# Forming a layer's expert sums in expert rows and scattering them to the tokens, in a two-layer attention and expert kernel

## The chip, the cores and the metric

The kernel runs on one core of one Trainium2 chip. The metric is the device time of one launch in microseconds, as the median of several runs. A profile is one execution of the same program, taken by the hardware profiler. The engines are called PE (TensorE, the matrix unit), DVE (VectorE), ACT (ScalarE), POOL (GpSimd) and SP (SyncE, which only issues transfers). Each of them carries out its own instructions in order, and waits in place when an operand is not there yet.

## The reference

800 tokens (8 batches of 100) of 512 numbers pass through four stages, each added to `x`: causal attention, experts with GELU, attention over tokens and context, and experts with SiLU. The change concerns the two expert stages, cut here to what counts:

```python
# layer 0
xf = xn.reshape(-1, d)                                  # xn: layer norm of x
probs = softmax(xf @ Wg.T + bg)
tp, ti = top_k(probs, 2);  tp = tp / (sum(tp) + 1e-8)
h = gelu(einsum('td,efd->tef', xf, W1) + b1)
y = einsum('tef,edf->ted', h, W2) + b2
out = sum over the two experts of tp * y                # added to xn and to x

# layer 1
top_vals, top_idx = top_k(x @ w_router, 2);  rw = softmax(top_vals)
h = silu(x @ w_gate) * (x @ w_up)
y = h @ w_down
out = sum over the two experts of rw * y
out = (out - mean(out)) * rsqrt(var(out) + 1e-5)        # over the 512 numbers of a token
x = x + out * ln_gamma + ln_beta
```

Every token is computed by its two best experts out of eight; the sum needs both of its answers, and in layer 1 the norm needs the sum.

## The kernel before

The kernel lays 800 tokens out in seven tiles of 128 partitions, the first with 32 tokens (`rows`, `starts`, lines 71 and 72). It goes through attention 0, experts 0, attention 1 and experts 1.

*Routing* (`Route`, line 219). `group` finds the two best experts of a few tiles of tokens, ranks every token in its two experts and gives it a row in each: `where[0]` and `where[1]` are row numbers in a table of 8 x 800 rows. The tokens are then scattered by indirect transfers into `sent`, a table of that shape in DRAM. `order` (line 292) sorts the experts by their load. Slot 0 of the loop that follows is the expert with the most tokens, and so on; `slot` holds each expert's slot.

*The loop over experts* (`work_off`, line 397). Eight slots run one after the other with capacities of 256, 240, 228, 220, 204, 200, 184 and 176 rows. For each slot, `arrived` fetches its rows from `sent` in two pieces on GpSimd's queue (`xg`), and TensorE turns them (`ps_tp`). `hidden1` (line 980) computes eight pieces of the hidden layer, each from 4 matmuls into `ps_g` and 4 into `ps_u`, ScalarE's SiLU, and VectorE's product `h` (line 995). The PSUM tiles `ps_g` and `ps_u` have two buffers each. After the first four pieces `between()` calls `send_back` of the slot before. `products` (line 366) then runs 64 matmuls into `ps_y`; the first eight of them need the eight pieces of `h` one after the other. `returned` (line 386) turns the answers back (`ps_yt`), copies them by VectorE to `y` and writes them to the table `answers` in DRAM in two pieces on GpSimd's queue. The second write waits for the first, since both address the table by a row known only at run time.

*Weights.* Pieces of 1 MB come on SyncE's queue into eight buffers (`Weights`, line 43). A piece is asked for as soon as a buffer is free: two when the first half of the hidden layer is done, two when the second is, two when the products are.

*What follows the loop.* If an expert has more tokens than its capacity, `rest` (line 412) works off the remainder under a branch. In layer 0 (lines 734 to 757) the part `project_early` projects five heads of context keys and values for the next attention, while for every token tile the two answers are fetched by indirect transfers (`fetch`, `back0`), added to `x` with their weights `m1` and `m2`, and the sum is normed (`moments`, `factors`, `scaled`) and turned into `xT1`, from which the next attention starts with `ps_col`. In layer 1 (lines 1019 to 1036) the two answers of each tile are fetched (`back1`), summed into `acc`, normed, multiplied by `gain`, added to `x`, which already has `bias` in it (line 967, in `fetch_gains`), and written to the output by SyncE.

The order of instructions on each engine is not the order of the source alone: a scheduler of the framework places them when the program is built. Transfers issued by GpSimd use eight completion semaphores in turn.

Of the kernel before, what the change touches and what calls it, by code (L numbers as in the profile page):

```python
# [38 lines left out]
GROUPS = ((0, 2), (2, 4), (4, 6), (6, NTILE))  # L39
SHORT = NT - NT // P * P  # L40
# [26 lines left out]
def two_layers(ctx: ExitStack, tc: tile.TileContext, a: dict, out: bass.AP):  # L67
# [144 lines left out]
    answers = dram.tile([ROWS, D], F32, name="answers")  # L212
    kept_keys = dram.tile([len(KEPT), P, S], F32, name="kept_keys")
# [5 lines left out]
    class Route:  # L219


        def __init__(self, layer, psum, tag):
            self.layer, self.psum, self.tag = layer, psum, tag
            self.logits = routes.tile([P, NTILE, NE], F32, tag="logits", name=f"logits{layer}")
            nc.vector.memset(self.logits, 0.0)
            self.m = [routes.tile([P, NTILE], F32, tag=f"m{k}", name=f"m{k}_{layer}") for k in range(2)]
            self.where = [
                routes.tile([P, NTILE], mybir.dt.int32, tag=f"where{k}", name=f"where{k}_{layer}") for k in range(2)
            ]
            self.sel = routes.tile([P, NTILE, NE], F32, tag="sel", name=f"sel{layer}")  # L230
            nc.vector.memset(self.sel[:, 0, :], 0.0)
            self.before = routes.tile([P, NTILE + 1, NE], F32, tag="before", name=f"before{layer}")
            nc.vector.memset(self.before[:, 0, :], 0.0)
# [4 lines left out]
        def largest(self, v, m, name):  # L238

            g = v.shape[1]  # L240
            nc.vector.tensor_reduce(m, v, AX.X, ALU.max)
            at = self.temp([P, NTILE, NE], f"at{name}")[:, :g, :]
            nc.vector.tensor_tensor(at, v, over_experts(m), ALU.is_equal)
            nc.vector.tensor_tensor(at, at, rank.unsqueeze(1).to_broadcast([P, g, NE]), ALU.mult)
            first = self.temp([P, NTILE], "first")[:, :g]
            nc.vector.tensor_reduce(first, at, AX.X, ALU.max)
            nc.vector.tensor_tensor(at, at, over_experts(first), ALU.is_equal)
            return at

        def group(self, i0, i1, xn, held=()):  # L250
# [3 lines left out]
            at1 = self.largest(v, self.m[0][:, i0:i1], 1)  # L254
            other = self.temp([P, NTILE, NE], "other")[:, :g, :]
            nc.vector.scalar_tensor_tensor(other, at1, -3e38, v, ALU.mult, ALU.add)
            at2 = self.largest(other, self.m[1][:, i0:i1], 2)
# [16 lines left out]
            for k, at in enumerate((at1, at2)):  # L274
                pick = self.temp([P, NTILE, NE], "pick")[:, :g, :]
                nc.vector.tensor_tensor(pick, at, row, ALU.mult)
                place = self.temp([P, NTILE], "place")[:, :g]
                nc.vector.tensor_reduce(place, pick, AX.X, ALU.add)
                nc.vector.tensor_copy(self.where[k][:, i0:i1], place)
# [12 lines left out]
        def order(self, load):  # L292
# [7 lines left out]
            slot = self.temp([P, NE], "slot")  # L300
# [29 lines left out]

    def rows_of(table, layer, s, r, n):

        of_all = table.rearrange("(e r) d -> e r d", e=NE)
        return of_all[bass.ds(owner[layer][s], 1), r : r + n, :].rearrange("o r d -> (o r) d")
# [13 lines left out]

    def fetch(dst, where, i, k):
        w = rows[i]  # L350
        nc.gpsimd.indirect_dma_start(
            out=dst[:w, :], out_offset=None,
            in_=answers, in_offset=bass.IndirectOffsetOnAxis(ap=where[k][:w, i : i + 1], axis=0),
        )
# [42 lines left out]
    def work_off(jobs, arrive, hidden, product, send_back, first=None, midway=None):  # L397


        (x, raw), done = arrive(*jobs[0][:3]), None  # L400
        if first is not None:
            weights.load(first + 8, raw[:1, 0, :1])
        for k, (e, r0, n, w1, w2) in enumerate(jobs):
            h = hidden(e, n, x, w1, lambda: done and send_back(*done))
            if k + 1 < len(jobs):
                x, raw = arrive(*jobs[k + 1][:3])
            if midway is not None and k == 4:
                midway(raw)
            done = e, r0, n, product(e, n, h, w2)
        send_back(*done)  # L410

    def rest(more, work, first, second, bufs):

        v = nc.values_load(more[:1, :1], min_val=0, max_val=1)
        with tc.If(v > 0), tc.tile_pool(name="rest", bufs=bufs) as rp:

            def piece(w):
                t = rp.tile([P, 4, 512], F32, tag="r", name="wr")
                nc.sync.dma_start(out=t, in_=w())
                return t  # L420

            work([
                (e, r0, min(CAP, NT - r0), lambda g, e=e: first(piece, e, g), lambda g, e=e: second(piece, e, g))
                for e in range(NE) for r0 in range(CAPS[e], NT, CAP)
            ])

# [61 lines left out]
    with tc.tile_pool(name="a0", bufs=1) as ap, tc.tile_pool(name="a0w", bufs=3) as aw, tc.tile_pool(  # L488
# [19 lines left out]
        def fill(table):  # L508
            flat = table.rearrange("r d -> (r d)").rearrange("(p f) -> p f", p=P)
            n = ROWS * D // P  # L510
            for k in range(0, n, 1024):
                nc.sync.dma_start(out=flat[:, k : min(n, k + 1024)], in_=nil[:, : min(1024, n - k)])
# [3 lines left out]
        fill(answers)  # L516
        weights.load(W_L0F)
# [164 lines left out]
        nc.vector.tensor_tensor(m2, m2, s, ALU.mult)  # L682


    with f0, tc.tile_pool(name="f0w", bufs=2) as fw, tc.tile_pool(
# [29 lines left out]
        def work0(jobs, first=None, midway=None):  # L715
# [3 lines left out]
                lambda e, r0, n, yT: returned(0, e, r0, n, yT, fp, ps), first, midway,  # L719
            )  # L720

# [7 lines left out]
        ], W_L0F, fetch_context)  # L729
        rest(  # L730
            more, work0, lambda piece, e, g: piece(of(0, "W1", e, g)), lambda piece, e, g: piece(of(0, "W2", e, g)), 4
        )

        bo = fw.tile([P, D], F32, name="bo", bufs=1)
        nc.scalar.dma_start(out=bo, in_=a["bo"][0].partition_broadcast(P))
# [6 lines left out]
        xT1 = columns_tile("xT1")  # L742
        for i in range(NTILE):
            w = rows[i]
            both = fp.tile([P, 2, D], F32, tag="nil", name="back0", bufs=2)
            for k, m in enumerate((m1, m2)):
                y = both[:, k]
                fetch(y, where, i, k)
                nc.vector.scalar_tensor_tensor(
                    x[:w, i, :], y[:w], m[:w, i : i + 1], x[:w, i, :], ALU.mult, ALU.add  # L750
                )
            xn = fp.tile([P, D], F32, tag="mv", name="xn1", bufs=2)
            scaled(xn, x[:, i, :], *factors(moments(x[:, i, :], "a1"), "b", twice=True))
            to_columns(xT1, xn, starts[i], rows[i], ps, gamma1, beta1)
            nc.gpsimd.tensor_tensor(x[:, i, :], x[:, i, :], bo, ALU.add)
        weights.limit = len(pieces)
        weights.load(W_L1A + 8, y[:1, :1])
# [197 lines left out]
    with tc.tile_pool(name="f1", bufs=1) as fp, tc.tile_pool(name="f1w", bufs=2) as fw, tc.tile_pool(  # L955
# [3 lines left out]
        acc = fp.tile([P, NTILE, D], F32, name="acc")  # L959

        def fetch_gains(behind):

            for t, n in ((gain, "ln_gamma"), (bias, "ln_beta")):
                nc.gpsimd.tensor_copy(t[:1, :1], behind[:1, 0, :1])
                nc.gpsimd.dma_start(out=t, in_=a[n].partition_broadcast(P))
            for i in range(NTILE):
                nc.gpsimd.tensor_tensor(x[:, i, :], x[:, i, :], bias, ALU.add)
            nc.gpsimd.tensor_copy(acc[:1, 0, :1], behind[:1, 0, :1])
            nc.gpsimd.memset(acc[:, 0, :], 0.0)
# [30 lines left out]
        def work1(jobs, first=None, midway=None):  # L1000
            work_off(
                jobs, lambda e, r0, n: arrived(1, e, r0, n, fw, ps), hidden1,
                lambda e, n, h, wd: products(n, h, [wd(g) for g in range(NF // 4)], NF, fw, ps),
                lambda e, r0, n, yT: returned(1, e, r0, n, yT, fw, ps), first, midway,
# [8 lines left out]
        ], W_L1F, fetch_gains)  # L1013
        rest(
            more, work1, lambda piece, e, g: (piece(of(1, "w_gate", e, g)), piece(of(1, "w_up", e, g))),
            lambda piece, e, g: piece(of(1, "w_down", e, g)), 2,
        )

        for i in range(NTILE):
            w = rows[i]  # L1020
            for k, m in enumerate((m1, m2)):
                y = fw.tile([P, D], F32, tag=f"back{k}", name="back1")
                fetch(y, where, i, k)
                if k == 0:
                    nc.vector.tensor_scalar(acc[:w, i, :], y[:w], m[:w, i : i + 1], None, ALU.mult)
                else:
                    nc.vector.scalar_tensor_tensor(
                        acc[:w, i, :], y[:w], m[:w, i : i + 1], acc[:w, i, :], ALU.mult, ALU.add
                    )

        for i in range(NTILE):
            w = rows[i]
            scaled(acc[:, i, :], acc[:, i, :], *factors(moments(acc[:, i, :], "out"), "a"))
            nc.vector.tensor_tensor(acc[:, i, :], acc[:, i, :], gain, ALU.mult)
            nc.vector.tensor_tensor(x[:, i, :], x[:, i, :], acc[:, i, :], ALU.add)
            nc.sync.dma_start(out=y_out[starts[i] : starts[i] + w], in_=x[:w, i, :])
# [70 lines left out]
```

## Time and profile before

| | us |
|---|---|
| median of 3 runs | 1853.74 (1853.73 to 1857.28) |
| the profiled execution's own time | 1852.47 |
| its span in the profile | 1851.0 |
| experts of layer 0, and the attention's start after them | 252 to 634, then 689 |
| experts of layer 1, first `ps_g` to last `ps_yt` | 1513.8 to 1804.1 |

The page's table of engines gives, for each, the microseconds in which it was busy and the number of instructions. Timelines list, in order of time, start, length, engine, line of the kernel, operation, output and inputs, how many were merged, and in brackets how long the engine stood idle before and what ended that. The busy time of 40 slices shows where the holes lie:

```profile
PE   4999899999999969999999999999999959999990
PEclk9999899999999979999999999999999979999995
```

A digit is the busy share in tenths of a slice of 46.3 us, in the second row the granted clock. The last slice, and the fifteenth, are the stretches after the two loops over experts.

### The profile page before, as it was taken

The page shows a single profiled execution, that of the slowest core. Times are in us where ns is not written, and L with a number is a line of the kernel's source. Part 1 is how long each engine was busy: PE and PEld are TensorE (multiplying, and loading weights), DVE is VectorE, ACT ScalarE, POOL GpSimd, SP SyncE. Part 2 cuts the span into 40 slices and gives each one's busy share as a digit, 9 for nine tenths or more (in the row PEclk, how much of TensorE's full clock was granted, in tenths as well). Part 3 has the DMA queues.
Part 4 walks back from the last instruction along what each step waited for, and adds up shares of the span by engine and source line. Part 5 has one row for each costly group of instructions (what it writes and reads, how often), then busy time and mean ns, then how long its engine had stood idle before and what let it go on. Part 6 is the DMA issues. An engine that isn't in the chain of part 4 may idle for free.

```text
span 1851.0 us, 26473 instructions
## 1 busy us (share of the span) xinstructions
PE 1725.6 (93%) x10427; PEld 1305.7 (71%) x10427; DVE 583.7 (32%) x1467; ACT 465.5 (25%) x1390; POOL 159.5 (9%) x266
## 2 busy tenths in 40 slices
PE   4999899999999969999999999999999959999990
PEld 2455578999999835566666656666666649999990
DVE  3464510101111050254454424444344411111115
ACT  2365321111111141343333323333233310010110
POOL 4010210000000040000010000000000010030003
PEclk9999899999999979999999999999999979999995
DMA  9921294454556373031120111213110255565513
GB/s 369 407 78 54 88 343 164 169 193 174 201 199 234 136 256 113 17 97 45 62 71 5 5 35 6 37 10 56 5 6 4 28 201 204 180 218 196 200 62 116
DMA packets 74485, 233.31 MB, mean 126 GB/s; under 512 B 23178, under 2 KB 35582, under 8 KB 57958
## 3 DMA queue, kind: packets, MB, share of 16 engines
q1 hardware_dynamic: 52978, 183.42, 29.0%
q0 software_dynamic: 10048, 30.58, 5.2%
q10 hardware_dynamic: 11316, 17.43, 3.2%
q8 instruction: 86, 1.41, 0.3%
q14 instruction: 57, 0.47, 0.1%
HBM read 180.36 MB, written 51.04 MB: 125 GB/s over the span
## 4 chain that ended last, share of the span: by engine, by line
PE 65%; issue 20%; DMA 10%; DVE 3%; ACT 1%; POOL 0%; POOLq 0%; ACTq 0%; another core or an unknown queue 0%; DVEq 0%
PE ps_m L443 17%; PE ps_col L432 7%; DMA answers<-y 6%; PE ps_sc L808 5%; PE ps_g L989 4%; PE ps_u L989 4%; PE ps_av L858 4%; PE ps_y L374 4%; PE ps_v L890 3%; PE ps_ptA L837 3%; PE ps_o L906 3%; PE ps_mv L455 2%; PE ps_v L535 2%; DMA back<-answers,where 1%; PE ps_o L646 1%
## 5 line engine op out<-in xcount | busy, mean ns | idle before, releaser
L443 PE MATMUL ps_m<-cb,w 128*128 128x361 f32 x896 | 297.3, 482 | 0.0
L374 PE MATMUL ps_y<-h,w 128*128 128x256 f32 (+7 forms) x1536 | 280.5, 344 | 0.0
L374 PEld LDWEIGHTS ps_y<-h,w 128*128 128x128 f32 x1536 | 268.6, 190 | 7.9
L443 PEld LDWEIGHTS ps_m<-cb,w 128*128 128x128 f32 x896 | 169.4, 194 | 102.1 <-issue 14.0
L706 PE MATMUL ps_h<-xgT,w 128*128 128x256 f32 (+7 forms) x1024 | 187.5, 344 | 0.0
L706 PEld LDWEIGHTS ps_h<-xgT,w 128*128 128x128 f32 x1024 | 179.2, 190 | 5.3 <-ACT h L710 0.2
L814 ACT ACTIVATE pr<-ps_sc,m 100x822 f32<-100x822 f32 x128 | 120.0, 943 | 188.1 <-DVE m L812 94.9
L812 DVE TENSOR_REDUCE m<-ps_sc 100x1 f32<-100x822 f32 x128 | 123.8, 1009 | 46.5 <-PE ps_sc L808 46.5
L838 DVE COPY prT<-ps_ptA 128x500 f32<-128x500 f32 x128 | 82.1, 678 | 168.5 <-PE ps_ptA L837 168.5
L447 ACT COPY mT<-ps_m 128x361 f32<-128x361 f32 x128 | 59.0, 462 | 299.2 <-PE ps_m L443 273.8
L710 ACT ACTIVATE h<-ps_h,s_b 128x256 f32<-128x256 f32 (+7 forms) x128 | 56.1, 439 | 303.5 <-PE ps_h L706 303.5
L432 PE MATMUL ps_col<-xT,w 128*128 128x400 f32 x320 | 115.1, 518 | 1.6 <-ACT xT L180 1.6
L989 PE MATMUL ps_g<-xgT,w 128*128 128x256 f32 (+7 forms) x512 | 103.1, 344 | 0.0
L989 PE MATMUL ps_u<-xgT,w 128*128 128x256 f32 (+7 forms) x512 | 102.8, 344 | 0.0
L432 PEld LDWEIGHTS ps_col<-xT,w 128*128 128x128 f32 x320 | 61.9, 197 | 48.0 <-issue 4.5
L808 PE MATMUL ps_sc<-mT,qT 64*100 64x311 f32 (+1 forms) x512 | 93.1, 468 | 0.0
L989 PEld LDWEIGHTS ps_u<-xgT,w 128*128 128x128 f32 x512 | 90.7, 190 | 2.6
L989 PEld LDWEIGHTS ps_g<-xgT,w 128*128 128x128 f32 x512 | 90.5, 191 | 2.7
L858 PEld LDWEIGHTS ps_av<-prT,mv 128*64 128x64 f32 (+1 forms) x1536 | 68.5, 138 | 27.9 <-issue 25.4
L994 ACT ACTIVATE sg<-ps_g 128x256 f32<-128x256 f32 (+7 forms) x64 | 22.3, 349 | 237.6 <-PE ps_g L989 237.5
L858 PE MATMUL ps_av<-prT,mv 128*64 128x100 f32 (+1 forms) x1536 | 81.2, 255 | 0.0
L837 PEld LDWEIGHTS ps_ptA<-ident,pr 100*128 100x128 f32 x640 | 65.2, 140 | 20.7 <-issue 10.6
(250 smaller groups left out, 1821.6 us busy)
## 6 DMA issues: line engine op xcount, KB each, us to landing
w<-in_W SPq DMA_DIRECT2D x64, 1024.0 KB
w<-in_w_gate SPq DMA_DIRECT2D x16, 1024.0 KB
w<-in_w_up SPq DMA_DIRECT2D x16, 1024.0 KB
w<-in_w_down SPq DMA_DIRECT2D x16, 1024.0 KB
sent<-nil SPq DMA_DIRECT2D x25, 512.0 KB
answers<-nil SPq DMA_DIRECT2D x25, 512.0 KB
cb<-in_ctxT ACTq DMA_DIRECT2D x16, 722.0 KB
mT<-kept_keys SPq DMA_DIRECT2D x13, 361.0 KB
```

Source lines behind the costliest of these rows:

```text
L374: nc.tensor.matmul(py[:, k, :n], ws[f // 4][:, f % 4, dc * P : (dc + 1) * P], h[:, f, :n], start=f == 0, stop=f == nf - 1,)
L432: nc.tensor.matmul(ps[:, :HALF], w[c // 4][:, dc, (c % 4) * P : (c % 4 + 1) * P], xT[:, dc, cols], start=dc == 0, stop=dc == DC - 1,)
L443: nc.tensor.matmul(pm[:, : S // 2], w_m[ic // 4][:, dc, (ic % 4) * P : (ic % 4 + 1) * P], cb[h][:, dc, : S // 2], start=dc == 0, stop=dc = ...
L447: nc.scalar.copy(mT[:, h * (S // 2) : (h + 1) * (S // 2)], pm[:, : S // 2])
L706: nc.tensor.matmul(ph[:, :n], w[:, dc, j * P : (j + 1) * P], xg[:, dc, :n], start=dc == 0, stop=dc == DC - 1,)
L808: nc.tensor.matmul(sc[:, bank, c0:c1], qT[r, ic, q0 : q0 + T], keys_, start=True, stop=True)
L812: nc.vector.tensor_reduce(m, sc[:, :, :NKH], AX.XY, ALU.max, negate=True)
L814: nc.scalar.activation(pr.rearrange("p (a n) -> p a n", a=2), sc[:, :, :NKH], AF.Exp, bias=m, accum_out=sums[:, j : j + 1],)
L837: nc.tensor.transpose(pt[:, c, :], pr[:, T + c * P : T + (c + 1) * P], ident[:T, :T])
L838: nc.vector.tensor_copy(prT[:, : NSC - 1, :], pt)
L858: nc.tensor.matmul(po[r, 0, :], vj, prT[j][:w, c, :], start=c == 0, stop=c == NSC)
L989: nc.tensor.matmul(p_[:, :n], w_[:, dc, j * P : (j + 1) * P], xg[:, dc, :n], start=dc == 0, stop=dc == DC - 1,)
```

## The change

Three things change.

*Layer 0.* After routing, `by_slot` exchanges the two experts of a token, its rows and its weights, so that index 0 is the one in the earlier slot. All first answers can then be fetched (`fetch_firsts`) while the last expert runs, and are added ahead of `project_early`; the second answers are all fetched after the loop. The square root of the norm moves from ScalarE to a power on GpSimd (`by_power=True`), every other tile is evicted by VectorE, and the adds of `bo` go behind the loop.

*Layer 1.* The tail after the loop is gone. During slot 0, `send_notes` scatters for each token and each of its experts a note of four numbers into the row that the token has there: the token's number if this is its later expert (otherwise a number past the end), the row of its other answer, and the two weights. `x` plus `bias` is written to a table `shifted` by tokens. For each later slot the notes are read (`read_notes`), and the other answer and the row of `shifted` are fetched by them (`summands`); the other answer is multiplied by its weight (`weighted`). When a slot's answers come back (`returned1`), VectorE adds the weighted answer from PSUM to the scaled other answer, for every row of the slot; `normed` forms the norm and the residual; and `sums_out` scatters the result to the output, leaving out rows whose token number is past the end. The copy to `y` goes from VectorE to ScalarE.

*The branch.* If it is taken, first answers and sums are done again (`again`).

```diff
+        def slots(self, behind):
+            wide = self.temp([P, NTILE, NE], "pick")
+            nc.gpsimd.tensor_copy(wide[:1, 0, :1], behind[:1, :1])
+            slots = [self.temp([P, NTILE], t) for t in ("key", "mine")]
+            for at, t in zip(self.at, slots):
+                nc.vector.tensor_tensor(wide, at, self.slot.unsqueeze(1).to_broadcast([P, NTILE, NE]), ALU.mult)
+                nc.vector.tensor_reduce(t, wide, AX.X, ALU.add)
+            return slots
+        def by_slot(self, behind):
+            slots = self.slots(behind)
+            swap = slots[0]
+            nc.vector.tensor_tensor(swap, slots[0], slots[1], ALU.is_gt)
+            for pair in (self.places, self.m):
...
@@ layer 0, the last expert and behind the loop
+        def fetch_firsts():
+            for i in range(NTILE):
+                fetch(firsts[i], where, i, 0)
-        ], W_L0F, fetch_context)
+        ], W_L0F, (4, fetch_context), fetch_firsts)
+        for i, w in enumerate(rows):
+            nc.vector.scalar_tensor_tensor(
+                x[:w, i, :], firsts[i][:w], m1[:w, i : i + 1], x[:w, i, :], ALU.mult, ALU.add
+            )
         for _ in project_early(
...
+        seconds = fw.tile([P, NTILE, D], F32, tag="h", name="seconds", bufs=1)
+        for i in range(NTILE):
+            fetch(seconds[:, i], where, i, 1)
         for i in range(NTILE):
...
-            scaled(xn, x[:, i, :], *factors(moments(x[:, i, :], "a1"), "b", twice=True))
-            to_columns(xT1, xn, starts[i], rows[i], ps, gamma1, beta1)
+            scaled(xn, x[:, i, :], *factors(moments(x[:, i, :], "a1"), "b", twice=True, by_power=True))
+            to_columns(xT1, xn, starts[i], rows[i], ps, gamma1, beta1, vector=i % 2 == 1)
@@ layer 1
+        def send_notes(behind):
             for t, n in ((gain, "ln_gamma"), (bias, "ln_beta")):
                 nc.gpsimd.tensor_copy(t[:1, :1], behind[:1, 0, :1])
                 nc.gpsimd.dma_start(out=t, in_=a[n].partition_broadcast(P))
+            slots = route.slots(behind[:, 0, :])
...
+            for i in range(NTILE):
+                for k in range(2):
+                    d = nc.gpsimd.indirect_dma_start(
+                        out=notes, out_offset=bass.IndirectOffsetOnAxis(ap=where[k][: rows[i], i : i + 1], axis=0),
+                        in_=note[: rows[i], k, i, :], in_offset=None,
+                    )
...
             for i in range(NTILE):
                 nc.gpsimd.tensor_tensor(x[:, i, :], x[:, i, :], bias, ALU.add)
+            nc.gpsimd.dma_start(out=shifted[:SHORT], in_=x[:SHORT, 0, :])
+            nc.gpsimd.dma_start(out=shifted[SHORT:].rearrange("(i p) d -> p i d", p=P), in_=x[:, 1:, :])
+            read_notes(1)
+        def read_notes(e):
+            for r in range(0, CAPS[e], P):
+                w = min(P, CAPS[e] - r)
+                n = fw.tile([P, 4], F32, tag="n", name="n", bufs=6)
+                nc.gpsimd.dma_start(out=n[:w], in_=rows_of(notes, 1, e, r, w))
+                read.setdefault(e, []).append((w, n))
+        def summands(e):
+            for w, n in read[e]:
...
+                gather(other[:w], answers, at[:w, 2:])
+                gather(base_[:w], shifted, at[:w, 1:2])
+        def weighted(e):
+            for (w, n), (_, _, other, _) in zip(read[e], ready[e]):
+                nc.vector.tensor_scalar(other[:w], other[:w], n[:w, 3:], None, ALU.mult)
+        def normed(acc, w, src):
...
+            nc.vector.bn_stats(st[:w], acc)
+            nc.vector.bn_aggr(mv[:w], st[:w])
+            nc.gpsimd.tensor_scalar(r[:w], mv[:w, 1:], EPS, None, ALU.add)
+            nc.gpsimd.tensor_tensor(r[:w], r[:w], half[:w], ALU.pow)
+            nc.vector.scalar_tensor_tensor(acc, acc, mv[:w, :1], gain[:w], ALU.subtract, ALU.mult)
+            nc.vector.scalar_tensor_tensor(acc, acc, r[:w], src, ALU.mult, ALU.add)
+        def sums_out():
+            for w, acc, base_, at in sums:
+                normed(acc[:w], w, base_[:w])
+                d = nc.gpsimd.indirect_dma_start(
+                    out=y_out, out_offset=bass.IndirectOffsetOnAxis(ap=at[:w, :1], axis=0),
+                    in_=acc[:w], in_offset=None, bounds_check=NT - 1, oob_is_err=False,
+                )
...
+        def returned1(e, r0, n, yT):
...
+                    nc.vector.scalar_tensor_tensor(acc[:w], pt, note_[:w, 2:3], other[:w], ALU.mult, ALU.add)
+                    sums.append((w, acc, base_, at))
+                y = fw.tile([P, D], F32, tag="mv", name="y", bufs=2)
+                nc.scalar.copy(y[:w], pt)
+                nc.gpsimd.dma_start(out=rows_of(answers, 1, e, r0 + s * P, w), in_=y[:w])
...
+            def send_back(e, r0, n, yT):
+                returned1(e, r0, n, yT)
+                if first is None:
+                    return
+                if e + 1 < NE:
+                    summands(e + 1)
+                    if e + 2 < NE:
+                        read_notes(e + 2)
+                else:
+                    sums_out()
+            def product(e, n, h, wd):
+                if first is not None and e > 0:
+                    sums_out()
+                    weighted(e)
+                return products(n, h, [wd(g) for g in range(NF // 4)], NF, fw, ps)
...
-        for i in range(NTILE):
-            w = rows[i]
-            for k, m in enumerate((m1, m2)):
-                y = fw.tile([P, D], F32, tag=f"back{k}", name="back1")
-                fetch(y, where, i, k)
...
-            nc.sync.dma_start(out=y_out[starts[i] : starts[i] + w], in_=x[:w, i, :])
```

## The prediction

> **What bounds the kernel now.** I read the table of engines first, then the chain of waits, then three timelines: the tail, the joint between the layers, and one expert of layer 1.
>
> ```profile
> span 1851.0 us, 26473 instructions
> PE 1725.6 (93%) x10427; PEld 1305.7 (71%) x10427; DVE 583.7 (32%) x1467; ACT 465.5 (25%) x1390; POOL 159.5 (9%) x266
> ```
>
> TensorE is the bound: time is won where it stands idle and lost where another engine makes it wait. The longest idle stretch is the tail; timeline rows (start, length, engine, operation):
>
> ```profile
> 1802.82 1.28 PE L392 MATMUL ps_yt<-ident,yT 128*128 128x128 f32 x8
> ...
> 1813.86 0.95 POOL L351 DMA_INDIRECT back<-answers,where  x1 [5.02 <-issue]
> ...
> 1846.80 0.69 DVE L1035 TENSOR_TENSOR x<-x,acc 128x512 f32<-128x512 f32 x1
> ```
>
> TensorE ends at 1804.1 and the span 46.9 us later. The joint is the second stretch:
>
> ```profile
> 641.71 4.42 PE L443 MATMUL ps_m<-cb,w 128*128 128x361 f32 x14
> ...
> 653.80 0.79 PE L455 MATMUL ps_mv<-ident,mT 128*128 128x128 f32 x4 [3.97 <-ACT mT L447]
> 654.38 4.80 PE L443 MATMUL ps_m<-cb,w 128*128 128x361 f32 x10
> ...
> 689.21 31.07 PE L432 MATMUL ps_col<-xT,w 128*128 128x400 f32 x83 [1.60 <-ACT xT L180]
> ```
>
> From the last products (633.8) to the first projection (689.2) it runs with holes, because ScalarE's evictions stand in order behind square roots that wait for fetched answers. Rows one and three also price a stall: 14 matmuls take 4.42 us, but after 3.97 us of idleness 10 take 4.80 instead of 3.16 (the granted clock was halved): 1.6 us lost per stall of that length.
>
> Between experts TensorE has no hole today. Expert 4 of layer 1, TensorE, GpSimd and SyncE rows:
>
> ```profile
> 1683.43 1.04 PE L392 MATMUL ps_yt<-ident,yT 128*128 128x128 f32 x8
> 1696.04 11.25 PE L374 MATMUL ps_y<-h,w 128*128 128x204 f32 x64
> 1685.06 0.56 POOL L395 DMA_DIRECT2D answers<-y  x1 [22.94 <-DVE y L394]
> 1692.23 0.54 POOL L395 DMA_DIRECT2D answers<-y  x1 [6.62 <-DMA answers<-y]
> 1696.50 1.17 POOL L362 DMA_DIRECT2D xg<-sent  x2 [3.72 <-PE ps_tp L171]
> 1694.16 1.71 SPq L58 DMA_DIRECT2D w<-in_w_down  x2
> ```
>
> The second write of answers waits for the first to land. Landing times asked window by window (size, us to landing): the first write of expert 3's answers in the burst of two weight pieces, the fetch of rows in the burst of `w_down`, and a write of the same size for expert 6, when no weights move:
>
> ```profile
> answers<-y POOLq DMA_DIRECT2D x1, 256.0 KB, 6.5
> xg<-sent POOLq DMA_DIRECT2D x1, 256.0 KB, 6.9
> xg<-sent POOLq DMA_DIRECT2D x1, 96.0 KB, 6.4
> answers<-y POOLq DMA_DIRECT2D x1, 256.0 KB, 2.3
> ```
>
> **The change part by part**
>
> *Tail.* Removed: 14 fetches at 1.26 us (1813.86 to 1831.2), seven norms on VectorE and the plain writes. Left, from 1804.1: two sums 0.75 each (row L1027), two statistics 0.69, two aggregates 0.17, two centrings 0.75, one final sum 0.75: 5.5 us, with gaps 1810. The two scatters need 2 x 1.26 and 3.7 us to land (median of the `back` fetches): 1816; with the branch, 2.6 us (the 5.02 above less a landing of 2.4), partly beside it, 1817. Gain **34** (30 to 36).
>
> *Joint.* The first answers are fetched during expert 7 of layer 0; GpSimd is free there and the write of expert 7's answers comes some 30 us later. Seven adds, 5.3 us, lie under `project_early`. The square roots leave ScalarE (GpSimd takes 0.22 + 0.57 us each, rows L147, L148), so the five heads run at the clean cadence of 6.4 us (635.3 to 641.7) from 641.7: the last transposes end at 667 rather than 674.7. Seven fetches begin at 646.3 as before and land by 658; the seven tiles are then evicted by two engines, ScalarE's four at 1.7 us: 676 against 689.2. Gain **13** (8 to 20; the upper end if the halved clock at 689 goes too). `by_slot` falls into VectorE's idle 14.8 us at 235.7; moving `bo` and its adds costs nothing, as they are read only at the output; SyncE's fill of `notes` lies under layer 0's attention. Without their covers these are 3, 9 and 1 us.
>
> *Experts 2 to 6 of layer 1.* VectorE runs in order, and the built kernel places the two scalings of `other` (`weighted`) ahead of the eighth `h` of the same expert. They wait for a fetch from `answers`, that for the second write, that for the first. Behind the scaling stands h8, and the eighth of 64 product matmuls waits for it. On GpSimd the two scatters of `out` precede the fetch, and they wait for two `pow` (0.57 each), which stand behind the second write. For expert 4: second write issued by 1692.8; first `pow` 1693.4, VectorE's sum 0.75, scatters 1694.2 to 1696.7 (1.26 each), fetches issued at 1696.7 and 1698.0, 5.8 us after the second write began. That is where the fetch of `xg` stands today, in the burst, with 6.4 us to land: 1704.4; scaling 0.48, h8 0.36: 1705.3. TensorE wants h8 at 1696.04 + 7 x 0.176 = 1697.3: **8.0 us of stall**. With each expert's own rows: 5.8, 7.3, 8.0, 7.6 and, for expert 6 (its second write itself lands in 5.9), 8.7: **37**. Each is longer than the 3.97 us above, so 1.6 to 1.8 for the clock: **9**. Moving the copy of `y` to ScalarE and the earlier place of the `xg` fetches cost nothing: both have an expert's length to spare. Ends: 10, if fetches land as without weights, and 53.
>
> Here a rule speaks for the change. The Trainium skill, *DMA: Bandwidth & Descriptors*, "Anatomy of one DMA", fits a GpSimd transfer as 2.0 us + bytes/436e3, so 2.6 us for 256 KB, and "Queues, rings and completion order" lets each DMA engine alternate between queues packet by packet, which at worst doubles the second term: 3.2. By the rule the first write lands by +4.8 from the transposes, the fetches by +14.6, h8 at +15.7 against +13.9 wanted: 2 us per expert, 10 in all and no clock loss. The rows say 6.5 and 6.4 to 6.9 in the bursts, 2.3 outside: the rule holds outside, not inside. I take the rows.
>
> *Experts 1 and 7.* The scaling waits on shorter chains: two scatters fewer in 1, no weights moving in 7. By the same sum 2 us each (0 to 5).
>
> *Expert 0.* `send_notes` puts on GpSimd 14 scatters of notes, seven adds of `bias`, two writes of `shifted` and the reads of notes; VectorE, after the fifth `h`, waits for the notes of experts 1 and 2, and before the eighth for those of expert 3, which stand behind four fetches of `base`. Today's rows for that work:
>
> ```profile
> 1635.06 8.63 POOL L967 TENSOR_TENSOR x<-x,bias 128x512 f32<-128x512 f32 x7 [2.59 <-DMA bias<-in_ln_beta]
> 1539.96 1.89 PE L989 MATMUL ps_u<-xgT,w 128*128 128x256 f32 x8
> ```
>
> The rows of expert 1 land by 1518.1 (6.8 us, as the fetch of 256 KB issued at 1513.54), `gain` and `bias` are asked for by 1520, notes 14 x 1.26 to 1537.6, adds to 1546.3, two writes to 1547.6, four reads (0.56 each) to 1549.9. These land behind 1.5 MB of `shifted`; the nearest is the context load by GpSimd, 4.8 to 5.9 us for 722 KB: 1554. VectorE's 16 small operations (0.17) end at 1557, then h6. TensorE needs h6's PSUM slot at 1539.96, its last `ps_u`. The fetches of `base` run to 1560, the reads for expert 3 are issued by 1561 and land at 1565, h8 at 1565.8; it is wanted at 1542.07 + 7 x 0.219 = 1543.6: **22** (12 to 28), and **2** for the clock after the second wait. With idle GpSimd this would be free; but a quarter of it is the adds, which today lie under expert 3 with nobody waiting.
>
> **Sum.** 22 + 2 + 2 + 37 + 9 + 2 = 74 lost among the experts, 34 + 13 = 47 won: +27 on the profiled execution's own 1852.5, so 1879.5. The median of the runs is 1.3 higher: **1880**.
>
> **Rivals**
>
> 1. *Bursts cost nothing (faster).* Landings by the rule above: experts 2 to 6 lose 10, expert 7 two, expert 0 still 20 (its wait is GpSimd's own work): 32 lost, 47 won, **1839**. For it: 2.1 to 2.7 us landings whenever no weights move, and DMA engines busy only 50 to 65% here. Against it: every row in a burst. It decides if the fetches land in under some 4 us and the first write in under 4.
> 2. *Half of it.* The first write is slow, as today, but the fetches need the 3.7 us of the `back` rows: 2.7 less per expert: 61 lost, **1868**.
> 3. *The clock stays down.* After the idle joint `ps_col` matmuls start 0.67 us apart until 695.5 and 0.336 after it: 6 us at half clock. If each stall of experts 2 to 6 halves the clock for the rest of its products, 10 us, 5 are lost rather than 1.7; with expert 0 at its 28: **1903**.
> 4. That overflow (`more`) is taken and the sums are made twice: not with these inputs, since the trace of before skips the branch.
>
> **How the numbers follow.** Forecast 0.55, rival 1 0.13, rival 2 0.22, rival 3 0.10. The forecast's own range is 1868 to 1896. The range of 8 in 10 runs from 1850, above rival 1 and below rival 2, to 1904. Within 0.2% (3.7 us), about what this kernel's runs can tell from no change, lie the edges of rivals 1 and 2: 0.03; faster 0.13; slower 0.84.
>
> **What would show it.** Right: VectorE's scaling of `other` waiting on DMA for 8 us or more per expert, `ps_y` of layer 1 waiting on h, half clock after each; a gap of some 17 us before the last `ps_u` of expert 0; the span ending some 13 us after the last `ps_yt`; `ps_col` starting near 676 on today's clock. Wrong: `ps_y` without gaps, or fetches of `other` landing within 4 us beside `w_down`.

## The result and the profile after

The changed kernel takes 1899.12 us (median of 4 runs, 1896.03 to 1902.31) against 1853.74: 1.0247 times as long, 95% interval 1.023 to 1.0264. It is slower by 45, where 26 was forecast. The profiled execution took 1896.03 us with a span of 1894.5, 43.5 more than before; the sums below are made against it.

The page's table of engines, then the busy tenths of 40 slices (TensorE, and the clock it was granted):

```profile
span 1894.5 us, 26754 instructions
PE 1742.9 (92%) x10427; PEld 1319.2 (70%) x10427; DVE 600.4 (32%) x1572; ACT 463.2 (24%) x1378; POOL 235.1 (12%) x368
...
PE   5999899999999979999999999999999569888884
...
PEclk9999899999999979999999999999999779999997
```

The empty last slice is gone. In its place most slices of layer 1's experts show 8 instead of 9, the one of expert 0 shows 6, and the clock there 7. Who waited for whom on TensorE, from expert 0 of layer 1 to the end (us in total, times, longest):

```profile
PE ps_y L409 <- DVE h L1165: 37.4, 11, 7.4
PE ps_u L1159 <- DVE h L1165: 18.7, 4, 14.7
```

Before, the same stretch has no such row. 56 us of waiting for VectorE's `h` are new, in a stretch where VectorE is busy a fifth of the time: it isn't slow, it stands in front of something else. What each part of the span did:

| part | before | after | gain | forecast |
|---|---|---|---|---|
| start of layer 1's experts (first `ps_g`) | 1513.8 | 1502.8 | 11.0 | 13 |
| loop, first `ps_g` to end of last `ps_yt` | 290.3 | 370.0 | -79.7 | -74 |
| from there to the end of the span | 46.9 | 21.7 | 25.2 | 34 |

In the loop TensorE stood for 56.2 of the 370.0 us and worked for 313.8, against 290.3 without a hole before: the same matmuls took 23.5 us longer, at a mean granted clock of 0.92 instead of 1.00.

Expert 0 of the changed kernel in its timeline, VectorE and TensorE:

```profile
1522.68 0.42 DVE L1165 TENSOR_TENSOR h<-ps_u,sg 128x256 f32<-128x256 f32 x1 [3.03 <-PE ps_u L1159]
1543.56 0.15 DVE L1066 TENSOR_SCALAR to<-n 128x1 f32<-128x1 f32 x1 [20.45 <-DMA n<-notes]
...
1545.38 0.76 DVE L1165 TENSOR_TENSOR h<-ps_u,sg 128x256 f32<-128x256 f32 x2
1545.86 3.78 PE L1159 MATMUL ps_u<-xgT,w 128*128 128x256 f32 x8 [14.65 <-DVE h L1165]
```

After the fifth `h` VectorE waits 20.45 us for the notes, and TensorE 14.65 us for the sixth. Expert 3 (rows of VectorE, GpSimd and TensorE):

```profile
1682.14 0.38 DVE L1165 TENSOR_TENSOR h<-ps_u,sg 128x220 f32<-128x220 f32 x1
1688.09 0.17 DVE L1069 CAST at<-to 128x2 int32<-128x2 f32 x1 [5.57 <-DMA out<-acc,at]
...
1689.27 0.37 DVE L1165 TENSOR_TENSOR h<-ps_u,sg 128x220 f32<-128x220 f32 x1
1691.45 0.48 DVE L1079 TENSOR_SCALAR other<-other,n 128x512 f32<-128x512 f32 x1 [1.81 <-DMA other<-answers,at]
1693.31 0.48 DVE L1079 TENSOR_SCALAR other<-other,n 92x512 f32<-92x512 f32 x1 [1.37 <-DMA other<-answers,at]
1693.71 0.38 DVE L1165 TENSOR_TENSOR h<-ps_u,sg 128x220 f32<-128x220 f32 x1
...
1684.85 1.02 POOL L383 DMA_INDIRECT other<-answers,at  x1 [0.30 <-issue]
1686.18 1.22 POOL L383 DMA_INDIRECT other<-answers,at  x1 [0.30 <-issue]
...
1689.70 0.64 PE L409 MATMUL ps_y<-h,w 128*128 128x220 f32 x2 [2.39 <-DVE h L1165]
1694.14 11.72 PE L409 MATMUL ps_y<-h,w 128*128 128x220 f32 x50 [3.81 <-DVE h L1165]
```

The last row is the forecast stall: the eighth `h` (1693.71) stands behind the two scalings of `other`, these wait for the fetches, and the fetches land 6.6 and 7.1 us after their issue. The second row is one that was not forecast: the seventh `h` stands behind the writing of a new index tile `at`, which waits until the scatter of `out` that reads the old one has landed. From 1540 us on, VectorE waited longer for such scatters than for the fetches (us in total, times, longest):

```profile
DVE at L1069 <- DMA out<-acc,at: 41.0, 8, 11.3
DVE other L1079 <- DMA other<-answers,at: 22.8, 14, 5.4
```

### The profile page after: what moved, and what is told of

Read it like the earlier page. It is cut to its first block, busy times and chain, and to the rows that moved or that the text cites. A ratio compares the mean times of both kernels' runs of the same rounds, so it can differ in the third digit from the quotient of the medians.

```text
span 1894.5 us, 26754 instructions
## 1 busy us (share of the span) xinstructions
PE 1742.9 (92%) x10427; PEld 1319.2 (70%) x10427; DVE 600.4 (32%) x1572; ACT 463.2 (24%) x1378; POOL 235.1 (12%) x368
## 4 chain that ended last, share of the span: by engine, by line
PE 45%; issue 26%; DMA 9%; POOL 3%; ACT 1%; DVE 1%; POOLq 0%; ACTq 0%; DVEq 0%
PE ps_m L480 14%; PE ps_sc L863 5%; PE ps_col L469 5%; DMA answers<-y 4%; PE ps_av L913 4%; PE ps_v L945 3%; PE ps_ptA L892 3%; PE ps_o L961 3%; PE ps_y L409 2%; PE ps_mv L492 2%; DMA firsts<-answers,where 1%; PE ps_g L1159 1%; DMA other<-answers,at 1%; PE ps_u L1159 1%; ACT pr L869 1%
## 5 line engine op out<-in xcount | busy, mean ns | idle before, releaser
L409 PE MATMUL ps_y<-h,w 128*128 128x256 f32 (+7 forms) x1536 | 297.7, 357 | 37.4 <-DVE h L1165 37.4
L409 PEld LDWEIGHTS ps_y<-h,w 128*128 128x128 f32 x1536 | 280.7, 198 | 50.4 <-DVE h L1165 41.2
L867 DVE TENSOR_REDUCE m<-ps_sc 100x1 f32<-100x822 f32 x128 | 123.8, 1008 | 46.6 <-PE ps_sc L863 46.6
```

What stands on the lines that cost most here:

```text
L409: nc.tensor.matmul(py[:, k, :n], ws[f // 4][:, f % 4, dc * P : (dc + 1) * P], h[:, f, :n], start=f == 0, stop=f == nf - 1,)
L867: nc.vector.tensor_reduce(m, sc[:, :, :NKH], AX.XY, ALU.max, negate=True)
```

## The experiments

"Time per expert" below is from its first `ps_g` to that of the next (for e7: to its first `ps_yt` behind the products), in the profiled execution. The kernel before ran again beside each experiment, at medians of 1851.0 to 1853.1 us, and the change did not; so differences to the change of two or three microseconds say nothing.

| kernel | e0 | e1 | e2 | e3 | e4 | e5 | e6 | e7 |
|---|---|---|---|---|---|---|---|---|
| before | 42.1 | 40.6 | 38.6 | 37.3 | 34.7 | 34.4 | 31.8 | 29.5 |
| the change | 67.0 | 41.5 | 47.6 | 46.9 | 47.0 | 44.1 | 41.3 | 33.5 |
| late | 68.2 | 40.6 | 47.6 | 47.1 | 46.6 | 37.6 | 40.3 | 29.5 |
| convert | 44.7 | 42.1 | 48.4 | 47.6 | 44.2 | 43.9 | 42.6 | 31.8 |
| nodep | 66.2 | 45.3 | 48.0 | 45.5 | 43.4 | 43.2 | 40.3 | 29.8 |
| noweights | 63.7 | 40.6 | 39.7 | 39.7 | 40.3 | 36.0 | 32.6 | 31.7 |
| best1 | 51.7 | 40.6 | 38.6 | 37.3 | 36.7 | 35.7 | 34.0 | 30.0 |
| best3 | 45.0 | 40.6 | 38.6 | 37.3 | 34.7 | 34.4 | 31.8 | 29.5 |

**joint: layer 0's part alone.** The layer-1 part of the file, from the pools `f1` on, is that of the kernel before:

```diff
-        ], W_L1F, (0, send_notes))
+        ], W_L1F, (4, fetch_gains))
```

> Only layer 0's part of the change; layer 1 with its tail is as before. Queue theory (what the change costs are waits behind other work in an engine's own order, all of them in layer 1): the gain of the joint stands alone, 11 us as in the changed kernel's profile (first ps_g of layer 1 at 1502.8 instead of 1513.8), so 1842 to 1844. Rival (the joint's gain is a time loan: the clock or the weights' transfers take it back in attention 1): 1849 or more.

Measured: 1845.57 us beside 1851.03, 0.9964 of the kernel before (0.995 to 0.9978), some 6 us won. Layer 1's experts start at 1505.1, 8.7 earlier, and each takes the time it took before (expert 0: 42.5). So the joint's gain stands on its own and no loss of the change comes from layer 0; the time is 2 to 4 us above what I expected. In both kernels with the new joint the same hole is to be seen (the changed kernel's timeline; ACTq is ScalarE's own DMA issue):

```profile
657.86 9.65 ACTq L502 DMA_DIRECT2D kept_values<-mv  x2
667.62 0.82 ACT L484 COPY mT<-ps_m 128x361 f32<-128x361 f32 x2 [9.62 <-DMA w<-in_Wkv]
...
668.13 1.54 PE L492 MATMUL ps_mv<-ident,mT 128*128 128x128 f32 x6 [6.61 <-ACT mT L484]
...
681.19 66.52 PE L469 MATMUL ps_col<-xT,w 128*128 128x400 f32 x192 [1.60 <-ACT xT L181]
```

The first row merges two writes. In *best2*'s expectation, below, I read it as an issue that takes 9.65 us; the raw records of the trace, with the semaphores that each transfer signals and each engine waits for, say otherwise (start, ns):

```
ScalarE DMA_DIRECT2D     657.86  327   kept_values, signals semaphore 106
SyncE   DMA_DIRECT2D     659.35  475   w, signals semaphore 107
ScalarE EVENT_SEMAPHORE  667.21   17   waits for semaphore 107
ScalarE DMA_DIRECT2D     667.27  252   kept_values, signals semaphore 107
```

Each write is issued in 0.3 us. Between them ScalarE waits 9.0 us, because the second is given the completion semaphore that a weight piece in flight has yet to signal; it does so by 667.2. The four pieces are asked for behind the last fetched answers, now at 658.6 and not at 673.5, and so come in between; TensorE waits 6.6 us for the eviction behind the second write. In *joint* the same semaphore holds the second write from 660.2 to 669.4.

**late: the other answer is scaled when the slot comes back.**

```diff
-                    weighted(e)
@@ returned1
-   nc.vector.scalar_tensor_tensor(acc[:w], pt, note_[:w, 2:3], other[:w], ALU.mult, ALU.add)
+   nc.vector.tensor_scalar(acc[:w], pt, note_[:w, 2:3], None, ALU.mult)
+   nc.vector.scalar_tensor_tensor(acc[:w], other[:w], note_[:w, 3:], acc[:w], ALU.mult, ALU.add)
```

> The other answer is no longer scaled ahead of time: VectorE scales the returned answer from PSUM and then adds the other answer times its weight, both when the slot's answers come back, one expert later. Nothing ahead of the eighth h waits for the fetch of the other answer any more. Queue theory: the waits of the eighth h (3.6, 3.8 and more per expert 2 to 7) go, those of the sixth and seventh h (notes, and the index tile that a scatter still reads: 2.4 to 2.9 per expert) stay, expert 0 stays: about 20 us less than the change, 1876 (1870 to 1882). Rival (the wait only moves: with the scaling gone the seventh h ends as late): 1890 or more. Rival (it is the clock, not the waits): no difference, 1897.

Measured: 1885.89, 1.0192 of before (1.0172 to 1.0213). 13 us less than the change, not 20; in the profiled runs the loop is 11.4 us shorter, nearly all of it in experts 5 and 7; experts 2 to 4 are as slow as they were. VectorE's rows of expert 3 show why:

```profile
1685.06 0.17 DVE L1069 CAST at<-to 128x2 int32<-128x2 f32 x1 [4.06 <-DMA out<-acc,at]
...
1690.73 0.17 DVE L1069 CAST at<-to 76x2 int32<-76x2 f32 x1 [5.16 <-DMA out<-acc,at]
...
1690.87 0.37 DVE L1166 TENSOR_TENSOR h<-ps_u,sg 128x220 f32<-128x220 f32 x1
```

No scaling stands before the eighth `h` any more, but the index tile does, and its scatter lands at about the time at which the fetch did. Two chains of nearly one length end at the same instruction, so removing one wins little: of experts 2 to 6 the first rival was right for all but expert 5.

**convert: the conversions of the notes on GpSimd.** In `summands`, and likewise for its three other conversions:

```diff
-   nc.vector.tensor_copy(at[:w, :2], to[:w])
+   nc.gpsimd.tensor_copy(at[:w, :2], to[:w])
```

> The four small conversions per piece of notes (token numbers and rows to integers) go from VectorE to GpSimd, which issues the fetches that need them. Nothing on VectorE waits for the notes any more. Queue theory: the whole stall of expert 0 goes (67.0 us from its first to the next expert's first matmul, against 42.1 before), in experts 2 to 6 the eighth h still waits for the scaling, so the time is 25 us less than the change, 1872 (1868 to 1876). Rival (half of expert 0's stall is GpSimd's own work and the traffic of 1.5 MB, whoever waits for it): 1884 or more. Below 1866 the conversions also held the experts 2 to 6.

Measured: 1873.3, 1.0129 of before (1.0081 to 1.0176): 26 us less than the change, as expected. Expert 0 takes 44.7 us instead of 67.0, with the same scatters, adds and 1.5 MB of writes under it. These cost TensorE next to nothing; what cost was that VectorE waited for them. Experts 2 to 6 keep their stalls: now the index tile waits on GpSimd, and the scaling still waits on VectorE. Either chain alone suffices.

**nodep: the two writes of answers not ordered behind one another.**

```diff
-   nc.gpsimd.dma_start(out=rows_of(answers, 1, e, r0 + s * P, w), in_=y[:w])
+   d = nc.gpsimd.dma_start(out=rows_of(answers, 1, e, r0 + s * P, w), in_=y[:w])
+   tc.declare_no_dep(d.ins, group="answers1", reason="rows differ")
+   tc.add_to_no_dep_group("answers1", d.ins)
```

> The changed kernel, but a slot's two writes of answers are no longer ordered behind one another (they go to different rows). Chain theory (eighth h, scaling, fetch of the other answer, scatters, norm's power on GpSimd, second write, landing of the first write): the second write goes out some 5 us earlier and everything behind it, so experts 2 to 6 lose 4 us less each, 20 in all: 1877 (1870 to 1884). Rival (the fetch itself, 6 to 7 us to land, and the scatters set the end): less than 8 us gained, 1890 or more.

Measured: 1890.36, 1.0216 of before (1.0192 to 1.0241), 9 us less than the change (7 if each is set against the kernel before beside it): the rival's range. In expert 3 both writes go out one after the other, and the two fetches 4.3 us earlier than in the change, counted from the transposes: at 1682.3 and 1683.6. But VectorE's row says

```profile
1693.02 0.48 DVE L1079 TENSOR_SCALAR other<-other,n 92x512 f32<-92x512 f32 x1 [6.58 <-DMA other<-answers,at]
```

The second fetch landed 9.4 us after its issue, where 7.1 were seen in the change: half of what was gained ahead of it was lost in flight. The edit also changed the built order: the fetches now stand ahead of the scatters, and the seventh `h` too stands behind both scalings. So this run doesn't price the second write alone.

**noweights: the same waits, without the bursts.**

```diff
+        weights.limit = W_L1F + 12
-   k=W_L1F + 6 * e
+   k=W_L1F + 6 * min(e, 1)
```

> The changed kernel, but experts 2 to 7 of layer 1 use the weights of expert 1, which stay in their buffers: no weight pieces move after expert 1's (left out: the right weights for those experts; instructions, sizes and waits are the same). Burst theory (the waits of the eighth h are long because writes and fetches land in 6 to 7 us beside weights): landings of 2.5 to 3.7 us, the stall of experts 2 to 6 falls from 6.2 to 9.3 us to at most 2.5 each, and the time to 1858 (1850 to 1866). Rival (the chain of GpSimd's own issues makes the stall, weights or not): stalls of 5 us or more stay, and 1880 or more.

Measured: 1856.43 (one run), as expected. Experts 2 to 6 lose 11.5 us to the kernel before, in sum, instead of 49.9, 8.5 of them standing. In layer 1's experts the instructions of VectorE, ScalarE and GpSimd and their order are the same, so 38 of the 50 us are due to the weights' transfers. It is the landing that they delay: here the second write of answers goes out 3.1 to 3.7 us after the first, with weights 6.4 to 7.3. The rest is the chain's own length. The scalings of expert 3 now wait 1.5 and 2.7 us:

```profile
1676.92 0.65 DVE L1079 TENSOR_SCALAR other<-other,n 128x512 f32<-128x512 f32 x1 [1.53 <-DMA other<-answers,at]
1680.22 0.48 DVE L1079 TENSOR_SCALAR other<-other,n 92x512 f32<-92x512 f32 x1 [2.66 <-DMA other<-answers,at]
```

**nobranch and tailsp: the end.** In the changed kernel's timeline TensorE's and GpSimd's last rows are

```profile
1871.48 1.29 PE L1114 MATMUL ps_yt<-ident,yT 128*128 128x128 f32 x8
...
1880.75 0.92 POOL L1099 DMA_INDIRECT out<-acc,at  x1 [0.30 <-issue]
```

and from 1881.7 to 1894.5 no view shows anything. *nobranch* and *tailsp* take away what could fill it:

```diff
@@ nobranch
-        rest(
-            more, work1, lambda piece, e, g: (piece(of(1, "w_gate", e, g)), piece(of(1, "w_up", e, g))),
...
@@ tailsp, the last expert in sums_out
+                if plain:
+                    nc.sync.dma_start(out=shifted[r * P : r * P + w], in_=acc[:w])
+                    continue
```

> The changed kernel without the branch for overflow after layer 1 (left out: the work for experts with more tokens than their capacity, which these inputs don't need). Theory: the last scatter is issued by 1881.7 in the changed kernel's profile and lands 2.8 us later, but the span ends at 1894.5; skipping the branch costs the 9 us between, which nothing covers now: 1888 (1886 to 1890). Rival (the scatters end late, or the end of a program costs this much after an indirect write): no difference, 1895 to 1899.

> The changed kernel, but the last expert's two sums are written by SyncE to a scratch table in plain rows, not scattered by GpSimd to the output (left out: the output rows of the tokens whose later expert is the last). In the changed kernel 12.8 us lie between the end of the last scatter's issue and the span's end, without the branch 8.9, where the kernel before has 3.2 us after its last write by SyncE. Theory (a GpSimd scatter takes 6 us more until the program can end): about 7 us between the last write's issue and the span's end, 6 less than the change. Rival (it is GpSimd's end of program, whatever it sent last): still 12 to 13 us.

Measured: nobranch 1900.34 (1.0268 of before, 1.0243 to 1.0292), above both ranges that I had set, with 8.9 us between the last scatter's issue and the span's end. So the branch is worth 3.9 of the 12.8. The span didn't fall because expert 1 took 48.9 us in the profiled execution and not 41.5, with the same instructions in the same order: its first write of answers and its fetches landed so late that the products had a hole of 6.5 us there, where the change's profile has 0.7. Whether that is so in the other three runs isn't shown. tailsp 1900.98 (one run), with 13.4 us after its last write: the rival, the scatter isn't it. The raw records of the trace, which the views leave out, name the rest (engine, instruction, start, ns; line 1269 is the launch):

```
before      GpSimd DRAIN            1829.87  5957
the change  GpSimd EVENT_SEMAPHORE  1882.80    17   line 451, the branch
            GpSimd INC_SWDGE_SEM    1883.37  2151   line 451
            GpSimd DRAIN            1885.56  8074   line 1269
            all    EVENT_SEMAPHORE  1893.82         the end of the program
```

GpSimd's closing instruction runs for 8.1 us after its last transfer. Before, it ran from 1829.9 to 1835.8, under VectorE's norms, 15 us ahead of the end. In nobranch it ran for 10.4 us, 8.1 of them behind the last scatter's issue.

**pooltail: the kernel before, its last write issued by GpSimd.** 

```diff
-            nc.sync.dma_start(out=y_out[starts[i] : starts[i] + w], in_=x[:w, i, :])
+            (nc.gpsimd if i == NTILE - 1 else nc.sync).dma_start(out=y_out[starts[i] : starts[i] + w], in_=x[:w, i, :])
```

> The kernel before, but its very last write of output is issued by GpSimd and not by SyncE. Theory (a program whose last work is GpSimd's ends some 6 us later than one that ends with SyncE, because GpSimd's own end takes some 9 us, which lay hidden behind the norms of the tail): the span ends 9 us after that write's issue and not 3.2, so 1857 (span 5 to 7 us longer). Rival (only indirect transfers or the branch make the end late): 1851 to 1853.

Measured: 1852.17 (one run, beside 1852.26), the rival's range. The span ends 4.9 us after that write's issue, not 9 as I expected and not 3.2 as before; GpSimd's closing instruction took 4.6 us here, some 4.0 of them after the issue. So the 9 us that I took for a constant of GpSimd's end are none: 4 us where GpSimd had been idle for 17 us before one write, 8 us after the scatters. What sets the length stays open.

**best1, best2, best3: all named waits away.** best1 joins late, convert and nodep, and reads the first notes ahead of the adds of `bias` in the source (the built order puts five of the seven adds in front all the same). best2 also asks for attention 1's weights later. best3 also ties the last step of the sum to the products:

```diff
@@ best2
-        weights.load(W_L1A + 8, seconds[:1, NTILE - 1, :1])
+        weights.load(W_L1A + 8, xn[:1, :1])
@@ best3, normed, called behind products
+   if yT is not None:
+       nc.vector.scalar_tensor_tensor(r[:w], yT[:w, DC - 1, :1], 0.0, r[:w], ALU.mult, ALU.add)
    nc.vector.scalar_tensor_tensor(acc, acc, r[:w], src, ALU.mult, ALU.add)
```

> All waits that the runs so far named are taken away together: other answer scaled late, conversions of notes on GpSimd, the two writes of answers not ordered behind one another, the notes of the first slot read ahead of the adds of bias. Queue theory: layer 1's loop at 291 to 293 us as before the change (it is 370 in the change), the tail 23, the joint 8 to 11 won: 1820 (1814 to 1826). Rival (something else on the same queues is late next, as the fetch of rows or the sum's last step): 1830 or more.

> As the last one, and four weight pieces of attention 1 are asked for behind the last normed tile instead of the last fetched answers. In the changed kernel ScalarE's two writes of kept values take 9.65 us to issue at 657.9, in the burst of those weights, and TensorE waits 6.6 us for its next eviction. Theory: that hole goes, and 5 us more are won than by the last one: 1815 (1810 to 1821). Rival (the weights are then late for the attention): no difference or slower.

> As best2, but the last step of each sum (times the norm's factor, plus the row of shifted) is tied to the slot's products, so it no longer stands ahead of the seventh h. In best2 the products of experts 4 to 6 still wait 2.3, 0.8 and 1.8 us for that step, which waits for a power on GpSimd behind the fetches. Theory: those holes go, 4.8 us and 2.5 for the clock: 1821 (1817 to 1825). Rival (the step and its scatter then come late for the next expert): no gain or a loss.

Measured: best1 1834.68 (0.9901, 0.9884 to 0.9917), best2 1827.93 (0.9866, 0.985 to 0.9883), best3 1819.0 (0.9831, 0.9806 to 0.9857). best1 missed its 1820, as its rival said: something else was late next, in experts 4 to 6 and in expert 0. best2's 1815 was built on it and missed too; best3's 1821 held. For the former, VectorE in best2, expert 4:

```profile
1690.66 0.75 DVE L1091 SCALAR_TENSOR_TENSOR acc<-acc,r_out,base 92x512 f32<-92x512 f32 x1 [7.46 <-POOL r_out L1089]
1691.33 0.64 DVE L1168 TENSOR_TENSOR h<-ps_u,sg 128x204 f32<-128x204 f32 x2
```

The sum's last step stands ahead of the last two `h` and waits for a power that GpSimd issues behind the fetches. best3 moves it, and every expert from 1 to 7 is back at its time of before. Only the tail grew, from 23.1 us to 29.2: the last two sums of expert 6 now wait for the last products, and the sums of expert 7 for their scatters. best2's later weights won 6.7 us over best1: the hole at 661 is gone, `ps_col` starts at 674.5 and not at 681.5. With its waits gone the change wins 33 us, 7 of them by the later weights.

## Why the prediction came out as it did

The direction, the place and the mechanism were right; the loss was 17 us larger in the profiled execution (43.5 against 27). That the loop's terms came out so near is in part luck: TensorE stood for 56.2 us where I had 63, and its work took 23.5 us longer where I had 11 for the clock.

*Experts 2 to 6.* TensorE's holes there add up to 36.2 us, forecast 37. Right in sum, but not in its working, where two errors cancel. One made the stalls too long: each matmul of the source stands in the trace as two, so `products` is 32 matmuls and not 64, and the eighth `h` is wanted behind 14 records and not 7 (expert 3's products show 12, 2 and 50 around their two waits). That is 1.1 to 1.4 us per expert, so my own sum should have come to 31. The other made them too short: part of the holes (2.4 of 6.2 us in expert 3's products) stands before the seventh `h`, where the index tile waits for a scatter to land. I had counted the scatters' issue and not that their index tile is written again while they are in flight; and this second chain would have held the kernel had the first been absent (late). It also took over part of the first chain's waiting, so that the sign I had named, a scaling that waits 8 us or more, wasn't there: the longest was 5.4. The clock: 13.7 us (loss of 49.9 less holes), forecast 9: 2.4 to 3.0 us per expert rather than 1.6 to 1.8, at a granted clock of 0.92 to 0.93.

*Expert 0.* 24.9 us lost, forecast 24, but otherwise divided: TensorE stood for 17.2 us, forecast 22, and lost 7.6 by a granted clock of 0.81, forecast 2. The sixth `h` came 42.6 us after the first `ps_g`, forecast 43.2; so GpSimd's queue was timed well, and what TensorE lost at its low clock on the way (0.72 in the first 8 us) it did not have to wait. convert shows the cause as given: VectorE's conversions behind GpSimd's queue. Without that wait 2.6 us remain, all by the clock at the start (0.68); why it is lower there than before (0.97) stays open.

*Experts 1 and 7.* 0.9 and 4.0, forecast 2 each.

*The tail.* This term failed: 25.2 won, forecast 34. The scatters were issued 8.9 us after the last transposes (8.4 worked out). Behind them I put 4.5 us for landing and branch; it was 12.8. I had read the cost of a program's end off the old kernel, where GpSimd's closing instruction of 6 us lay hidden.

*The joint.* 11.0 won, forecast 13. The adds, fetches and square roots did as said; the term that was missing is the weights' request, which moved 15 us ahead with the answers that release it and into the semaphore of ScalarE's write. In best2, without it, `ps_col` starts at 674.5, forecast 676.

*The rivals.* That bursts cost nothing is refuted: fetches of `other` landed in 5.7 to 7.7 us in experts 2 to 5, and first writes in 5.7 to 6.7 in 2 to 6. The rule that I set against the rows (the Trainium skill, *DMA: Bandwidth & Descriptors*, "Anatomy of one DMA": a fixed 2.0 us and the bytes over 436e3) gave 10 us of stall for experts 2 to 6; in noweights they stood for 8.5, if unevenly (0.5 to 3.6). So in sum the rule comes near this chain when no weights move, and the rows of a burst when they do. Fetches of 3.7 us were seen in expert 6 alone (3.8); it stood for 7.0 us all the same, since both of its writes took 6.0 us or more. That the clock stays down came half true: 12.5 us more were lost by it than forecast.

Of the 17 us, 8.8 are the tail, 5.7 the loop (12.5 more by the clock, 7 less by standing) and 2 the joint. The median is 3 us above the profiled run; executions differ in how a write falls against a burst (expert 1: 41.5 us here, 48.9 in nobranch), which may be why.

## What to carry to other kernels

An operation that isn't needed until later costs nothing only if nothing urgent is queued behind it on its engine: look at the built order, and put the waits for transfers on an engine that has nothing to deliver. Count every chain that ends at the delayed instruction, reused index tiles and completion semaphores included, since removing one of two equal chains shows no gain, and take landing times from rows that share the moment's traffic. Work that moves to the end also uncovers what its engine does after it; look for what the old tail was hiding.

## What the runs showed of the hardware that was not expected

- GpSimd's closing instruction took 4.6 to 10.4 us and appears in no group or wait; a span whose end has no rows is worth a look at the raw records.
- Two engines' transfers shared a completion semaphore: ScalarE stood 9.0 us before a write that it issued in 0.25, until a weight piece of SyncE's had landed. The timeline's merged row shows that as one issue of 9.65 us; only what ended the wait (`w<-in_Wkv`) gives it away.
- In best1, best2, noweights and tailsp ScalarE and VectorE stood still in expert 0 for up to 12 us although their inputs were there. In best2's timeline

```profile
1523.28 0.66 ACT L1167 ACTIVATE sg<-ps_g 128x256 f32<-128x256 f32 x2 [12.21 <-remote]
...
1523.72 2.96 PE L1162 MATMUL ps_g<-xgT,w 128*128 128x256 f32 x8 [4.43 <-ACT sg L1167]
```

  ScalarE's next instruction is in the records only at 1523.28, though its matmuls ended at 1514.1. best2 lost 9.0 us in expert 0 (51.1 against 42.1), 4.4 of them standing; convert and best3, where neither engine stood still, lost 2.6 and 2.9. No run tried a cause, and it stays open.
